# Layer 3 of a four-layer kernel: PSUM banks divided 5/1/2 in place of 4/1/3, parameters in smaller steps, attention begun beside the first sequence's parameters

## The chip, the cores and the metric

The kernel runs on one core of one Trainium2 chip. The core has the engines PE (TensorE, matrix products; its weight loads are listed as PEld), DVE (VectorE), ACT (ScalarE), POOL (GpSimd) and SP (SyncE, which issues DMAs here). Each engine works through its own list of instructions in order and waits on semaphores for the others. Matrix products land in PSUM, which this program divides into eight banks of 128 x 512 f32; DVE and ACT read them from there.

The metric is the device time of one execution in microseconds (us). Before the change it is 3640.95 us, the median of three runs (3640.08 to 3649.79).

## The reference, cut to what matters

The kernel computes four layers, each `x = x + s * silu(ffn)`. The change touches layer 3 alone. It takes 8 sequences of 512 tokens with 128 features and computes two branches from the same normalized input:

```
xn = layernorm(x)
# branch s: state space mixer, 4 heads of 64, state 128
z, x, B, C, dt, A, trap, angles = split(xn @ W_in)
a = min(-softplus(A), -1e-4); dt = softplus(dt + dt_bias)
theta = cumsum(angles * dt)                 # over tokens
K = rope(rmsnorm(B) + B_bias, theta); Q = rope(rmsnorm(C) + C_bias, theta)
y = within a chunk: (Q K^T * g * decay) x  +  Q exp(ell) state   # plus D * x
s = (y * silu(z)) @ W_out
# branch ffn: attention, 16 heads of 8
attn = softmax over queries of (k q^T / sqrt(128)); out = sum_k attn * v
f = gelu(l2norm(l2norm(out @ Wo) @ Wff))
x = x + s * silu(f)
```

## The kernel before

Layer 3 works through the sequences one after another. A sequence has T = 512 tokens, JT = 4 tiles of 128.

**Attention in units.** A unit is one group of four heads (of four groups) and one tile of 128 keys, so a sequence has U = 16 units. `scores` makes four products of 128 x 512 on PE (L1957), each into a PSUM bank of the kind `pu`; DVE takes each product's negative maximum (`nm`, L1960), ACT its exponential with the sum of a row (L1961). Two units later (LAG = 2) `weigh` takes the reciprocal of the sums on DVE (L1934), scales the values on POOL (L1935) and makes four products into the single `pf` bank (L1942). After the fourth key tile of a group, the result is copied to `oT`.

**The mixer.** `mixer(b, jt)` handles one tile of 128 tokens. It is a generator of seven steps: (1) the z and x projection (L1849), tanh and copy on ACT, keys and queries with bias on POOL (L1858), rotation on DVE (L1863 to L1865); (2) the decay product (L1870) with four exponentials (L1875) and causal masking on POOL; (3, 4) four transposes each (L1889) and their copies; (5) the product of queries and keys (L1894), multiplied into E by DVE (L1895), and the new state (L1900, L1903 to L1906); (6) the output product with E (L1911) into the first half of the tile `py`, added to y by DVE (L1912), then the product with the state (L1915) into the second half of the same tile, scaled and added (L1917, L1918), times z (L1920); (7) two transposes (L1924) and a copy into `yT`.

**Beginning, parameters, end.** `begin(b)` normalizes, transposes and projects a sequence (L1723 to L1735) and then runs `parameters`, which computes softplus, decays, norms and angles for the whole sequence. Its steps are: two projections of two tiles each (L1754 to L1760); softplus and the products up to L1783; and everything else, from L1788 over the norms (L1800), the dot products (L1804 to L1815) and the cumulative angles (L1819, L1821) to sine and cosine (L1826 to L1839). `end(b)` multiplies by W_out (L1970) and Wo (L1980), normalizes, multiplies by Wff (L1996), applies gelu and writes the result.

**Banks.** The eight banks are divided by `k.banks("l3p", pu=4, pf=1, pa=3)`: four for scores, one for `weigh`, three in turn (`pa`) for all other products.

**What sets the order.** PE's instructions stand in the order in which the program makes them (`manual_schedule` for PE). A scheduler orders those of the other engines by data and priority; scores and weighing are made with high priority (`AHEAD`). The loop in `layer3` runs over the units n. In each it makes the scores, then one step of half of the running generators, then weighs unit n - 2, then one step of the other half:

```
if u == 0 and b + 1 < B:
    running.append(L.begin(b + 1))
mb, mu = divmod(n + HEAD, U)
if mb < B and mu % 4 == 0 and (mb, mu) != (0, 0):
    running.append(L.mixer(mb, mu // 4))
```

`begin(0)` with its parameters runs to its end ahead of the loop. A mixer starts every fourth unit, four units ahead of its place (`HEAD = 4`); `end(b)` starts after the last weighing of its sequence, first in the list.

Of the kernel before, what the change touches and what calls it, by code (L numbers as in the profile page):

```python
# [20 lines left out]
P = 128  # L21
# [1593 lines left out]
def softplus(nc, pool, x):  # L1615

    shape = list(x.shape)
    tl = lambda name: pool.tile(shape, F32, name=name)
    e, z, q, p = tl("sp_e"), tl("sp_z"), tl("sp_q"), tl("sp_p")
    nc.scalar.activation(e, x, AF.Abs)  # L1620
    nc.scalar.activation(e, e, AF.Exp, scale=-1.0)
    nc.vector.tensor_scalar(z, e, 2.0, None, ALU.add)
    nc.vector.reciprocal(z, z)
    nc.vector.tensor_tensor(z, z, e, ALU.mult)
    nc.vector.tensor_tensor(q, z, z, ALU.mult)
    nc.vector.tensor_scalar(p, q, 1.0 / 17, None, ALU.mult)
    for n in range(15, 1, -2):
        nc.vector.scalar_tensor_tensor(p, p, 1.0 / n, q, ALU.add, ALU.mult)
    nc.vector.scalar_tensor_tensor(p, p, 1.0, z, ALU.add, ALU.mult)
    nc.vector.tensor_scalar(x, x, 0.0, None, ALU.max)  # L1630
    nc.vector.scalar_tensor_tensor(x, p, 2.0, x, ALU.mult, ALU.add)


class Layer3:
# [69 lines left out]
    def begin(self, b):  # L1704


        k, nc, cn, fn, tp = self.k, self.k.nc, self.cn, self.fn, self.tp
        bt = slice(b * JT, (b + 1) * JT)
        xn = tp.tile([P, JT, C], F32, name="xn3", bufs=1)
        self.layernorm(self.x[:, bt, :], xn)  # L1710
        yield
        xT = tp.tile([P, T + 1], F32, name="xT3")
        nc.gpsimd.memset(xT[:, T:], 0.0)
        k.to_features(xn, xT, nt=JT)
        yield
# [10 lines left out]
        nc.tensor.matmul(ps, fn["Wq"], xT[:, 0:T], start=True, stop=True)  # L1726
# [12 lines left out]
        yield  # L1739
        yield from self.parameters(q)  # L1740

    def parameters(self, q):
# [8 lines left out]
        for jt in range(JT):  # L1751
            o = slice(jt * P, (jt + 1) * P)
            ps = k.pa()
            nc.tensor.matmul(ps[:, 0 : 256 + NPAR], xT[:, o], cn["bcp"], start=True, stop=True)  # L1754
            c0 = 256 + NPAR
            nc.tensor.matmul(ps[:, c0 + 4 : c0 + 4 + 2 * HM], xT[:, o], self.wm, start=True, stop=True)

            nc.tensor.matmul(ps[:, c0 : c0 + 4], xT[:, jt * P + 1 : (jt + 1) * P + 1], cn["trap"], start=True, stop=True)
            nc.scalar.copy(raw[:, jt].rearrange("p a n -> p (a n)"), ps[:, 0:256])
            nc.vector.tensor_copy(par[:, jt, :], ps[:, 256 : c0 + 4 + 2 * HM])  # L1760
            if jt % 2:
                yield

        beta = sm("beta3", 2, JT, HM)
        nc.scalar.activation(beta[:, 0], par[:, :, 8:12], AF.Tanh, scale=0.5)
# [4 lines left out]
        dt, a = sp[:, 0], sp[:, 1]  # L1770
        nc.vector.tensor_tensor(dt, par[:, :, 0:4], bc(cn["dt_bias"], 1, JT), ALU.add)
        nc.vector.tensor_copy(a, par[:, :, 4:8])
        softplus(nc, self.sp2, sp.rearrange("p a b c -> p (a b c)"))
        ad = ap.tile([P, JT, HM, NA], F32, name="ad3")
        nc.vector.tensor_tensor(ad, bc(par[:, :, 12:44], 2, HM), bc(dt, 3, NA), ALU.mult)
        src = ad.rearrange("p j h n -> p j (h n)")
# [5 lines left out]
        nc.vector.tensor_tensor(v["coef"], dt, beta[:, 1], ALU.mult)  # L1782
        nc.vector.tensor_tensor(v["c"], v["coef"], v["d"], ALU.add)  # L1783
        yield

        ps = k.pa((P, 3, JT * HM))
        for n, tri in enumerate((k.upto, k.above, k.ones)):
# [2 lines left out]
            nc.scalar.activation(flat(v[name]), ps[:, n, :], AF.Exp)  # L1790
        nc.vector.tensor_scalar(flat(v["ell"]), ps[:, 0, :], -1.0, None, ALU.mult)
        nc.vector.tensor_tensor(v["eout"], v["eout"], v["c"], ALU.mult)

        r = self.rms(raw.rearrange("p j a n -> p (j a) n"), 2 * JT, 1e-5)
        rv = r.rearrange("p (j a) -> p j a", a=2)
        BC = tp.tile([P, JT, 2, C], F32, name="BC3")
        nw = cn["nw"].rearrange("p (a n) -> p a n", n=C)
        for jt in range(JT):
            for w in range(2):
                nc.vector.scalar_tensor_tensor(  # L1800
                    BC[:, jt, w, :], raw[:, jt, w, :], rv[:, jt, w : w + 1], nw[:, w, :], ALU.mult, ALU.mult
                )
        prod = ap.tile([P, JT, C], F32, name="prod3")
        nc.vector.tensor_tensor(prod, BC[:, :, 0, :], BC[:, :, 1, :], ALU.mult)  # L1804
        dot = sm("dot3", JT)
# [7 lines left out]

        nc.vector.tensor_tensor(v["coef"], v["coef"], kqd, ALU.mult)
        nc.vector.tensor_tensor(v["coef"], bc(cn["D"], 1, JT), v["coef"], ALU.subtract)  # L1815

        W = JT * HM * NA
        ps = k.pa((P, JT, HM * NA))
# [19 lines left out]
        nc.scalar.activation(n, n, AF.Square)  # L1838
        nc.vector.tensor_scalar(of(cos), n, -2.0, 1.0, ALU.mult, ALU.add)  # L1839
        q.update(v=v, BC=BC, sin=sin, cos=cos, state=None)  # L1840
        q["yT"] = tp.tile([P, 2, JT, P], F32, name="yT3", bufs=1)

    def mixer(self, b, jt):

# [62 lines left out]
            q["state"] = new  # L1907
        yield
        py = k.pa((P, 2, HM, HP))
        for h in range(HM):  # L1910
            nc.tensor.matmul(py[:, 0, h, :], E[:, h, :], xc[:, h, :], start=True, stop=True)  # L1911
        nc.vector.tensor_tensor(y, y, py[:, 0], ALU.add)  # L1912
        if state is not None:
            for h in range(HM):
                nc.tensor.matmul(py[:, 1, h, :], kqT[:, 1, h, :], state[:, h, :], start=True, stop=True)  # L1915
# [12 lines left out]
    def weigh(self, b, u):  # L1928
# [34 lines left out]
    def end(self, b):  # L1963

        k, nc, cn, fn, tp, q = self.k, self.k.nc, self.cn, self.fn, self.tp, self.q.pop(b)
        s = tp.tile([P, JT, C], F32, name="s3", bufs=1)
        ps = k.pa((P, JT, C))
        for jt in range(JT):
            for w in range(2):
                nc.tensor.matmul(  # L1970
                    ps[:, jt, :], q["yT"][:, w, jt, :], cn["W_out"][:, w * C : (w + 1) * C],
                    start=(w == 0), stop=(w == 1),
                )
        nc.scalar.copy(s, ps)
        yield
        z = tp.tile([P, JT, C], F32, name="zo3", bufs=1)
        ps = k.pa((P, JT, C))
        for qt in range(JT):
# [4 lines left out]
                )  # L1983
        nc.scalar.copy(z, ps)
        yield
        r = self.rms(z, JT, 1e-12, floor=True)
        nc.vector.tensor_tensor(z, z, bc(r, 2, C), ALU.mult)
        yield
# [23 lines left out]
def layer3(k, x, A, at):  # L2012

    with ExitStack() as ctx:
        ctx.enter_context(k.banks("l3p", pu=4, pf=1, pa=3))
        L = Layer3(k, ctx, x, A, at, k.out)
        ctx.enter_context(k.tc.manual_schedule(engines={mybir.EngineType.PE}))
        for _ in L.begin(0):
            pass
        U = 4 * JT  # L2020
        AHEAD = 300
        HEAD = 4
        running = [L.mixer(0, 0)]
        for n in range(B * U + LAG):
            b, u = divmod(n, U)
            steps = iter(running)

            def step(share):

                for _ in range(share):  # L2030
                    w = next(steps, None)
                    if w is not None and next(w, False) is False:
                        running.remove(w)

            if b < B:
                if u == 0 and b + 1 < B:
                    running.append(L.begin(b + 1))
                mb, mu = divmod(n + HEAD, U)
                if mb < B and mu % 4 == 0 and (mb, mu) != (0, 0):
                    running.append(L.mixer(mb, mu // 4))  # L2040
                steps = iter(list(running))
                half = (len(running) + 1) // 2
                with k.tc.high_priority(offset=AHEAD):
                    L.scores(b, u)
                step(half)
            else:
                half = 0
            if n >= LAG:
                wb, wu = divmod(n - LAG, U)
                with k.tc.high_priority(offset=AHEAD):  # L2050
                    L.weigh(wb, wu)
                if wu == U - 1:
                    running.insert(0, L.end(wb))
            step(len(running))
        while running:
            for w in list(running):
                if next(w, False) is False:
# [87 lines left out]
```

## Time and profile before

| What | us |
|---|---|
| median of three runs | 3640.95 |
| profiled execution, whole time | 3647.2 |
| span of its records | 3645.5 |
| layer 3, first record of its constants' load to the end | from 2627.5 |
| first score of layer 3 (L1957) starts | 2669.4 |
| last unit's scores start | 3613.4 |

Over the whole span PE is busy 77% of the time, DVE 64%, ACT 45%, POOL 20%; these are means over four different layers. A row of the stage table gives the busy time of each engine in one stretch of the span, and the clock that PE was granted there as a share of full speed. A matmul's end is modelled, so PE's busy time in a group of products includes short waits inside the group. In a wait, the engine that stood is named first, then the one whose work it was waiting for, with the total, the number of times and the longest.

### The profile page before, as it was taken

To read this page: it belongs to the slowest core of one execution; us is meant where nothing else is said; L and a number is where in the kernel's file an instruction comes from. 1 tells how busy PE (TensorE), PEld (TensorE's weight loads), DVE (VectorE), ACT (ScalarE), POOL (GpSimd) and SP (SyncE) were. 2 spreads that over 40 slices of the span, in tenths; PEclk is the share of its full clock that TensorE was granted. 3 is DMA by queue.
4 is the path that set the end of the run, shared out by engine and by line. 5 is a ranking of instruction groups with operands and counts; after the bars stand their busy time and mean duration, and the time that the engine had idled before them with its cause. 6 is when DMAs were issued, how large, how long until landed. Compare 5 with 4: busy or idle time off the path is not lost.

```text
span 3645.5 us, 44996 instructions
## 1 busy us (share of the span) xinstructions
PE 2815.7 (77%) x16390; PEld 1512.3 (41%) x16390; DVE 2315.1 (64%) x6346; ACT 1645.2 (45%) x3211; POOL 743.0 (20%) x845
## 2 busy tenths in 40 slices
PE   6173657512998897799999999999678789887987
PEld 4142445302444454344444444443344445444543
DVE  7989898997582334334544544444467777777775
ACT  5162546512544445233333333333245566665665
POOL 0004040400225553101101101101121222222221
PEclk9585757555789999799999999998868889888988
DMA  4003030311002222000000000000000000000000
GB/s 119 2 2 71 1 82 1 72 48 34 1 2 50 41 39 41 42 1 1 1 1 1 1 1 1 1 1 1 21 1 1 4 4 1 4 3 4 1 4 7
DMA packets 67519, 64.53 MB, mean 18 GB/s; under 512 B 5344, under 2 KB 59616, under 8 KB 66784
## 3 DMA queue, kind: packets, MB, share of 16 engines
q1 hardware_dynamic: 39264, 42.75, 3.8%
q0 software_dynamic: 19712, 14.69, 3.1%
q10 hardware_dynamic: 8320, 4.19, 0.4%
q8 instruction: 129, 2.11, 0.2%
q14 instruction: 94, 0.77, 0.1%
HBM read 43.80 MB, written 17.83 MB: 17 GB/s over the span
## 4 chain that ended last, share of the span: by engine, by line
PE 36%; DVE 17%; ACT 7%; POOL 3%; issue 2%; DMA 1%; POOLq 0%; ACTq 0%; DVEq 0%; SPq 0%
PE pa L1372 6%; PE pu L1390 6%; DVE nm L1960 4%; ACT at L1961 3%; PE pu L1957 3%; PE pf L1942 2%; DVE mpad L1404 2%; PE pf L1435 2%; PE pa L1486 1%; PE pa L1485 1%; PE pa L1870 1%; ACT at L1422 1%; PE pa L1915 1%; DVE rope L1863 1%; PE pa L1509 1%
## 5 line engine op out<-in xcount | busy, mean ns | idle before, releaser
L1961 ACT ACTIVATE at<-pu,nm 128x512 f32<-128x512 f32 x512 | 348.1, 688 | 151.6 <-DVE nm L1960 125.1
L1960 DVE TENSOR_REDUCE nm<-pu 128x1 f32<-128x512 f32 x512 | 326.8, 680 | 66.6 <-PE pu L1957 66.5
L199 POOL TENSOR_SCALAR_AFFINE_SELECT at<-at 128x512 f32<-128x512 f32 x184 | 123.3, 670 | 1004.3 <-ACT at L1422 855.9
L1404 DVE TENSOR_REDUCE mpad<-pu 128x2 f32<-128x256 f32 (+3 forms) x256 | 199.2, 818 | 168.6 <-PE pu L1401 168.6
L1422 ACT ACTIVATE at<-pu 128x1024 f32<-128x1024 f32 (+3 forms) x256 | 171.7, 702 | 285.7 <-PE pu L1390 285.5
L1078 ACT ACTIVATE at<-pu,rsqrt 128x1024 f32<-128x1024 f32 (+3 forms) x256 | 190.9, 793 | 190.1 <-PE pu L1073 164.4
L1957 PE MATMUL pu<-qT,kT 32*128 32x512 f32 x1024 | 246.4, 703 | 6.0 <-ACT at L1961 5.1
L1372 PE MATMUL pa<-hid,f 128*128 128x512 f32 x512 | 222.7, 593 | 0.0
L1390 PE MATMUL pu<-qT,kT 32*128 32x512 f32 (+3 forms) x1024 | 160.8, 516 | 56.4 <-DVE mpad L1404 42.0
L748 PE MATMUL pa<-ident,Y 128*128 128x128 f32 x32 | 7.9, 426 | 210.9 <-DVE Y L739 210.9
L1390 PE MATMUL pu<-kT,qT 32*128 32x128 f32 (+3 forms) x1024 | 151.8, 569 | 14.4 <-ACT at L1422 10.2
L1942 PE MATMUL pf<-at,va 128*32 128x512 f32 x1024 | 158.9, 698 | 1.4 <-POOL va L1935 1.4
L548 POOL DMA_INDIRECT xg<-xn_d,idx x48 | 54.9, 1143 | 496.9 <-PE pf L552 316.3
L1372 PEld LDWEIGHTS pa<-hid,f 128*128 128x128 f32 x512 | 96.6, 190 | 119.5 <-issue 118.9
L1493 DVE SCALAR_TENSOR_TENSOR X<-X,u 128x512 f32<-128x512 f32 x56 | 38.7, 691 | 159.5 <-ACT u L1488 159.5
L1073 PE MATMUL pu<-qT,kT 32*128 32x512 f32 (+3 forms) x1024 | 131.1, 518 | 5.7 <-ACT at L1078 4.7
L1390 PEld LDWEIGHTS pu<-qT,kT 32*128 32x128 f32 x1024 | 67.5, 197 | 155.5 <-DVE mpad L1404 116.3
L1016 POOL DMA_INDIRECT f_d<-ys,idx x64 | 103.6, 1619 | 138.0 <-DMA f_d<-ys,idx 86.0
L1935 POOL TENSOR_TENSOR va<-V,sm 128x32 f32<-128x32 f32 x128 | 38.8, 303 | 451.7 <-DVE sm L1934 401.5
L1957 PEld LDWEIGHTS pu<-qT,kT 32*128 32x128 f32 x1024 | 81.9, 209 | 103.2 <-ACT at L1961 65.5
L1373 ACT ACTIVATE hid<-pa,f 128x512 f32<-128x512 f32 x64 | 44.0, 688 | 172.5 <-PE pa L1372 172.5
L1083 DVE TENSOR_TENSOR at<-at,ceiling 128x512 f32<-128x512 f32 x72 | 50.2, 698 | 108.2 <-ACT at L1078 104.8
(611 smaller groups left out, 6723.3 us busy)
## 6 DMA issues: line engine op xcount, KB each, us to landing
w<-in_w_dram SPq DMA_DIRECT2D x24, 512.0 KB, 3.8
f_d<-zeros ACTq DMA_DIRECT2D x8, 512.0 KB
xn_d<-xn SPq DMA_DIRECT2D x8, 512.0 KB, 4.9
w<-in_w_dram SPq DMA_DIRECT2D x16, 256.0 KB, 2.9
w<-in_w_dram SPq DMA_DIRECT2D x24, 128.0 KB
f<-in_f_dram SPq DMA_DIRECT2D x1, 2888.0 KB, 11.8
xn<-in_x_dram SPq DMA_DIRECT2D x4, 512.0 KB, 9.3
Gt<-in_x_dram SPq DMA_DIRECT2D x4, 512.0 KB
```

Of the source, the lines that this page charges most:

```text
L199: self.nc.gpsimd.affine_select(a, a if src is None else src, pattern, ALU.is_ge, 0.0, base=0, channel_multiplier=-1)
L1016: nc.gpsimd.indirect_dma_start(out=self.f_d, out_offset=bass.IndirectOffsetOnAxis(ap=idx[:, e, i : i + 1], axis=0), in_=ys[:, i, :], in_of ...
L1073: nc.tensor.matmul(pu[:, n, 0:m], q["kT"][r, g // 2, kc * P : kc * P + P], q["qT"][r, g, kc * P :], start=True, stop=True,)
L1078: nc.scalar.activation(at_[:, i : i + 2, 0:m], pu[:, :, 0:m], AF.Square, bias=k.rsqrt2, scale=32.0**-0.5)
L1372: nc.tensor.matmul(ps, fn[n][:, c0 : c0 + P], src[:, i, :], start=(i == 0), stop=(i == 3))
L1390: self.k.nc.tensor.matmul(pu[:, n, 0:m], a[r, c0 : c0 + P], b[r, q0 : q0 + m], start=True, stop=stop)
L1404: nc.vector.tensor_reduce(top[:, i : i + 2, 16], pu[:, :, 0:m], AX.X, ALU.max)
L1422: nc.scalar.activation(at_[:, i : i + 2, 0:m], pu[:, :, 0:m], AF.Exp, scale=8.0**-0.5)
L1942: nc.tensor.matmul(po[i * 32 : i * 32 + 32, :], va[:, kc, c0 : c0 + 32], E[:, i, :], start=(kc == 0), stop=(kc == JT - 1))
L1957: nc.tensor.matmul(pu, q["kT"][r, kc * P : (kc + 1) * P], q["qT"][r, g, :], start=True, stop=True)
L1960: nc.vector.tensor_reduce(nm[:, w], pu, AX.X, ALU.max, negate=True)
L1961: nc.scalar.activation(E[:, n, :], pu, AF.Exp, bias=nm[:, w], accum_out=sm[:, w])
```

## The change

Nothing is added to or taken from the computation. What is different:

- the banks are divided `pu=5, pf=1, pa=2`: scores go round five banks, the other products round two;
- `parameters` has more steps: softplus is a generator that yields after its two ACT instructions, further yields follow softplus, the products, the decays, half of and all of the norms, and the dot products; the reciprocal root for the norms (`rms`) is taken before softplus;
- in the mixer the product with the state comes ahead of the one with E; `yT` is allocated in the first mixer's last step in place of at the end of `parameters`;
- `end` makes the Wo product first, then waits until the last mixer has set `mixed`, then makes the W_out product;
- the loop starts as soon as the first sequence's projections stand (`ready`); the parameters of sequence 0 run as a generator beside the first units. Mixers are planned by `at`: from unit 10 on every third unit until they have caught up with their place, then every fourth, one unit ahead of it. `begin(b)` is planned for the later of the sequence's usual place and 16 units ahead of its first mixer, and not before the mixers that read its buffers.

```diff
     nc.scalar.activation(e, e, AF.Exp, scale=-1.0)
+    yield
     nc.vector.tensor_scalar(z, e, 2.0, None, ALU.add)
...
         yield
+        q["ready"] = True
         yield from self.parameters(q)
...
             if jt % 2:
                 yield
+        r = self.rms(raw.rearrange("p j a n -> p (j a) n"), 2 * JT, 1e-5)
...
-        softplus(nc, self.sp2, sp.rearrange("p a b c -> p (a b c)"))
+        yield from softplus(nc, self.sp2, sp.rearrange("p a b c -> p (a b c)"))
+        yield
...
         nc.vector.tensor_tensor(v["c"], v["coef"], v["d"], ALU.add)
+        yield
         yield
...
-        r = self.rms(raw.rearrange("p j a n -> p (j a) n"), 2 * JT, 1e-5)
+        yield
...
+            if jt == 1:
+                yield
+        yield
         prod = ap.tile([P, JT, C], F32, name="prod3")
...
         nc.vector.tensor_tensor(v["coef"], bc(cn["D"], 1, JT), v["coef"], ALU.subtract)
+        yield
...
-        q["yT"] = tp.tile([P, 2, JT, P], F32, name="yT3", bufs=1)
...
         py = k.pa((P, 2, HM, HP))
+        if state is not None:
+            for h in range(HM):
+                nc.tensor.matmul(py[:, 1, h, :], kqT[:, 1, h, :], state[:, h, :], start=True, stop=True)
         for h in range(HM):
             nc.tensor.matmul(py[:, 0, h, :], E[:, h, :], xc[:, h, :], start=True, stop=True)
         nc.vector.tensor_tensor(y, y, py[:, 0], ALU.add)
         if state is not None:
-            for h in range(HM):
-                nc.tensor.matmul(py[:, 1, h, :], kqT[:, 1, h, :], state[:, h, :], start=True, stop=True)
             inter = tl("inter3", HM, HP)
...
+        if jt == 0:
+            q["yT"] = self.tp.tile([P, 2, JT, P], F32, name="yT3", bufs=1)
...
         nc.scalar.copy(q["yT"][:, :, jt, :], ps)
+        q["mixed"] = jt
...
-        ctx.enter_context(k.banks("l3p", pu=4, pf=1, pa=3))
+        ctx.enter_context(k.banks("l3p", pu=5, pf=1, pa=2))
...
+        EARLY, EVERY = 10, 3
+        at = lambda b, jt: max(b * U + jt * JT - 1, EARLY + EVERY * (b * JT + jt))
...
+        for b in range(B):
+            if b:
+
+                read = at(b - 2, JT - 1) + 1 if b > 1 else 0
+                plan(max((b - 1) * U, at(b, 0) - U, read), lambda b=b: L.begin(b))
+            for jt in range(JT):
+                plan(at(b, jt), lambda b=b, jt=jt: L.mixer(b, jt))
+            plan(max((b + 1) * U + LAG, at(b, JT - 1) + 1), lambda b=b: L.end(b))
+        running = [L.begin(0)]
+        while not L.q or "ready" not in L.q[0]:
+            next(running[0])
+        for n in range(B * U + LAG + 1):
+            running.extend(make() for make in work.get(n, ()))
```

In `end` the W_out product and its copy move behind the Wo product, after

```diff
+        while q.get("mixed") != JT - 1:
+            yield
```

More of the change, by code (lines that the diff above doesn't have):

```diff
@@ L1965, in end @@
         k, nc, cn, fn, tp, q = self.k, self.k.nc, self.cn, self.fn, self.tp, self.q.pop(b)
[L1966 to L1975, printed above, removed]
         z = tp.tile([P, JT, C], F32, name="zo3", bufs=1)
@@ L1985, in end @@
         yield
+        while q.get("mixed") != JT - 1:
+            yield
+        s = tp.tile([P, JT, C], F32, name="s3", bufs=1)
+        ps = k.pa((P, JT, C))
+        for jt in range(JT):
+            for w in range(2):
+                nc.tensor.matmul(
+                    ps[:, jt, :], q["yT"][:, w, jt, :], cn["W_out"][:, w * C : (w + 1) * C],
+                    start=(w == 0), stop=(w == 1),
+                )
+        nc.scalar.copy(s, ps)
         r = self.rms(z, JT, 1e-12, floor=True)
@@ L2014, in layer3 @@
     with ExitStack() as ctx:
-        ctx.enter_context(k.banks("l3p", pu=4, pf=1, pa=3))
+        ctx.enter_context(k.banks("l3p", pu=5, pf=1, pa=2))
         L = Layer3(k, ctx, x, A, at, k.out)
         ctx.enter_context(k.tc.manual_schedule(engines={mybir.EngineType.PE}))
-        for _ in L.begin(0):
-            pass
         U = 4 * JT
         AHEAD = 300
[L2022 to L2026, printed above, removed]
+        EARLY, EVERY = 10, 3
@@ new lines, in layer3, with plan @@
+        at = lambda b, jt: max(b * U + jt * JT - 1, EARLY + EVERY * (b * JT + jt))
+        work = {}
+        def plan(n, make):
+            work.setdefault(n, []).append(make)
+        for b in range(B):
+            if b:
+                read = at(b - 2, JT - 1) + 1 if b > 1 else 0
+                plan(max((b - 1) * U, at(b, 0) - U, read), lambda b=b: L.begin(b))
+            for jt in range(JT):
+                plan(at(b, jt), lambda b=b, jt=jt: L.mixer(b, jt))
+            plan(max((b + 1) * U + LAG, at(b, JT - 1) + 1), lambda b=b: L.end(b))
@@ L2028, in step @@
+        running = [L.begin(0)]
[3 more added lines that the diff above has]
+            running.extend(make() for make in work.get(n, ()))
+            todo = list(running)
             def step(share):
-                for _ in range(share):
-                    w = next(steps, None)
-                    if w is not None and next(w, False) is False:
+                for w in todo[:share]:
+                    if next(w, False) is False:
@@ L2033, in step @@
                         running.remove(w)
[L2035 to L2042, printed above, removed]
-                with k.tc.high_priority(offset=AHEAD):
[L2044 to L2047, printed above, removed]
@@ L2048, in layer3 @@
-            if n >= LAG:
-                wb, wu = divmod(n - LAG, U)
+                del todo[:share]
+            if n < B * U:
+                with k.tc.high_priority(offset=AHEAD):
+                    L.scores(*divmod(n, U))
+                step((len(todo) + 1) // 2)
+            if LAG <= n < B * U + LAG:
                 with k.tc.high_priority(offset=AHEAD):
[L2051 to L2054, printed above, removed]
+                    L.weigh(*divmod(n - LAG, U))
@@ L2055, in layer3 @@
+            step(len(todo))
         while running:
```

## The prediction

> **What bounds the kernel now.** The change touches layer 3 alone, so I first looked for its stage. The stage table (busy us of each engine in stretches of the span) was read for the start of the layer, for one ordinary sequence and for the last one. Its columns are the stretch and its length, then busy time of PE, PEld, DVE, ACT and POOL, then granted clock, DMA share and GB/s.
>
> ```profile
> 2642.30:2669.40 27.10, 9.86 (x45) 7.27 (x43) 16.52 (x55) 5.83 (x15) 6.96 (x4) 0.62 0.00 0
> ...
> 2906.00:3024.00 118.00, 101.56 (x554) 54.17 (x554) 87.42 (x209) 75.15 (x192) 25.95 (x39) 0.84 0.01 3
> ...
> 3497.00:3616.00 119.00, 108.31 (x593) 55.44 (x594) 79.25 (x164) 73.55 (x201) 22.87 (x39) 0.88 0.01 3
> ```
>
> Between the first projections (2642.3) and the first score (2669.4) lie 27.1 us of parameters with no attention beside them. Each sequence then takes about 118 us for 16 units, 7.4 us a unit, and no engine is full: DVE 87 of 118, ACT 75, PE 102 at a clock of 0.84. The last sequence has no following parameters, less DVE work, and takes 119 all the same. So DVE's throughput is not the bound; waits that pass between engines are. The waits of the stage (2669.4 to 3616; total us, times, longest):
>
> ```profile
> PEld pu L1957 <- ACT at L1961: 65.5, 117, 3.3
> ...
> PE pa L1915 <- DVE y L1912: 50.1, 24, 3.3
> ...
> PE pa L1894 <- DVE coef L1814: 40.8, 3, 13.6
> ...
> PE pa L1849 <- DVE angle L1829: 29.0, 3, 9.8
> ```
>
> PE, whose order is the program's, stands 120 us at the last three places; the first line is its weight load for a score, which waits until an exponential frees the bank. What follows such a stand is seen in PE's timeline (start, us, line, operation; idle before it in brackets):
>
> ```profile
> 3062.30 1.13 PE L1726 MATMUL pa<-xT,f 128*128 128x512 f32 x2 [0.47 <-ACT s L1974]
> ...
> 3076.97 1.10 PE L1900 MATMUL pa<-xe,kq 128*128 128x64 f32 x8 [0.60 <-DVE par L1760]
> ...
> 3530.31 1.16 PE L1870 MATMUL pa<-upto,adt 128*128 128x128 f32 x8
> ...
> 3584.57 1.97 PE L1915 MATMUL pa<-state,kqT 128*128 128x64 f32 x8 [1.08 <-DVE y L1912]
> 3586.47 1.94 PE L1942 MATMUL pf<-at,va 128*32 128x512 f32 x8
> 3588.34 2.08 PE L1870 MATMUL pa<-upto,adt 128*128 128x128 f32 x8
> ```
>
> L1870 takes 1.16 us where PE did not stand, 2.08 soon after it did.
>
> **The change, part by part.** The instructions of PE, DVE and POOL are the same in number; only order and banks move.
>
> *A, earlier start.* Once qT and kT stand, the first scores are behind only two parameter tiles, at about 2645 in place of 2669.4: 24 us. The parameters' 16.5 us of DVE move beside units 0 to 9, which carry no mixer and need DVE 4 x 0.61 + 0.18 = 2.6 us each. The mixers postponed follow every third unit until unit 43, so their work is later, not gone. If DVE were the bound only its idle 27.1 - 16.5 = 10.6 us would be won, if nothing were, 24. Take **18**.
>
> *B, state product ahead of E product (L1915 before L1911).* Both write the tile py. Before, PE writes the first half, DVE reads it (L1912), and only then may PE write the second half. In the new order PE writes both and DVE comes after: the wait goes, 24 times 2.1 = 50 us. Late next is the product with E, whose input is made a unit earlier, and the transpose of y, which needs four DVE operations of about 0.41 (L1912, L1917, L1918, L1920), 1.6 us; between py and it PE has weights (1.06), a transpose group (0.66) and scores (1.1), 2.8 us, unless four maxima of 0.61 come first: 0 to 1 us each. The slow clock behind the stand: over the 24 places L1915 itself ran 11.8 us above 1.10 each, the L1942 after it 13 above 1.06, the L1870 15 above 1.13: 40 us. [...] The rows say 50 + 40 = 90, with half speed after gaps of 1.1 to 3.3 us. I use the rows, but not all of it: DVE and ACT do other work during the stand and have to keep up afterwards. **60**, bounds 25 and 90.
>
> *C, parameters in steps of a unit.* Before, everything from L1788 to the angles is one step; PE then finds a bank held by the angles' product until L1829 or a transpose not copied. That step's stands, all six of them, in the stage table (first two):
>
> ```profile
> 2859.50:2873.20 13.70, 0.07 (x5) 0.06 (x1) 12.25 (x31) 8.39 (x14) 2.36 (x3) 0.65 0.04 11
> 2985.90:2995.20 9.30, 0.00 (x0) 0.00 (x0) 8.18 (x19) 3.92 (x10) 3.68 (x3) 0.72 0.00 0
> ...
> sum 69.80, PE 0.10 PEld 0.12 DVE 61.99 ACT 37.33 POOL 19.66; mean PE 0.02 PEld 0.02 DVE 10.33 ACT 6.22 POOL 3.28
> ```
>
> PE does nothing for 69.8 us, but DVE works 62 of these, and that work remains. Spread over five units, with the softplus ahead of it over three, it must fit into the 31 us that DVE idles in a sequence. At least DVE's 8 us are won, at most 70. Take **35**.
>
> *D, fifth score bank.* A score then waits for an exponential five back, not four: 0.67 us earlier (688 ns of L1961 overlapping its 201 ns read). The 117 waits are 0.56 us on average, so nearly all 65.5 could go; but there ACT's four exponentials (2.7 us) set the pace in light units whatever the banks. **15**, bounds 0 and 50.
>
> *E, two banks for other products in place of three.* The stage takes 360 such tiles: 32 mixers x 7 + 24 state tiles = 248, beginnings 32, parameters 48, ends 32. With three banks PE's plain waits for them are small: 6.1 + 3.5 + 2.6 + 1.8 us in all (L1870 on xv, L1900 on par, L1754 on y, L1726 on s). With two, each tile waits for the last reader of the second before it. In the new PE order that is, in a mixer: the new state's product (L1900) behind z's tile (its readers tanh, DVE, copy ended 3.0 us after PE at 3550; 3.3 us of PE work lie between: 0 to 2); the decay product L1870 behind L1894's reader L1895 (0.68 alone, ended 3.2 us after PE at 3547; 1.0 us of PE between: 0 to 2.2). Take 0.5 each: 12 + 16 us. Parameter tiles in pairs 1 us, 16 in all: 16; the angles' tile 1.5 x 8 = 12; the tile of q with four readers of 0.7, 1.5 x 8 = 12. Sum 68. Queued behind each on PE are the next scores, for which DVE and ACT wait; half of it falls where PE would have waited for a score bank. **-35**, bounds 0 and -110.
>
> [...] The rows of short waits (0.47 and 0.60 us above) are followed by 1.13 and 1.10 us, full speed. [...]
>
> *F, small.* In the changed program's order ACT loads tables 36 times in the stage, before 40 times, 1.28 us each; off the path mostly: 2. At the end zo's product no longer stands behind s's (1.9 us), but the last mixer runs three units later with its transpose ahead: 0. Moving yT's allocation and the rms forward moves one POOL power of 1.64 us to an earlier unit; POOL is busy 26 of 118. No DMA is added; the one per sequence on SP moves with the ends.
>
> Sum: 18 + 60 + 35 + 15 - 35 + 2 = 95. The profiled execution took 3647.2 us (span 3645.5), so 3552; the median of the runs shown is 6 lower, 3641, and from it **3546**.
>
> **Rivals.** *R1, DVE becomes the bound:* the parameters' work only moves. A 10, B 25, C 8, D 0, E -20: 23 us, **3618**. For it: DVE works 90% of the stands. Against: 31 us idle a sequence, and the last sequence is no faster with 8 us less.
>
> *R2, the pair of banks becomes the bound, slower.* Place: L1870 and L1900 in each mixer, then the parameter tiles. It decides once the mean new wait is over 128 / 360 = 0.36 us a tile, since A to D and F give 130. Price at the upper ends: 32 x 2.2 + 24 x 1.5 + 40 of the others = 146, and slow groups after a third of them (30 us): 176 - 130 = 46 over, **3687**. For it: copies queue behind high priority maxima. Against: tiles of one mixer are mostly a unit apart.
>
> *R3, the stands go and nothing replaces them:* DVE's 715 us of the 1003 us from 2642 to the end (sums of the stage table) at 85% gives 841, 162 less: **3479**. For it: PE's work at full clock is an estimated 86 us a sequence, from the fast rows: scores 16 x 1.1, weights 16 x 1.06, mixers 4 x 7.6, end 7.7, parameters 9.3, beginning 4. Against: E.
>
> *R4, gains and new waits cancel:* within 11 us of 3641.
>
> **Chances.** Forecast 0.40 (own range 3505 to 3595), R3 0.20, R1 0.17, R4 0.05, R2 0.18. No change is within 0.3%, 11 us. Faster 0.76, same 0.06, slower 0.18. The range 3470 to 3660 leaves out about 0.05 below and 0.13 above.
>
> **What would show it.** A: first score near 2645. B: no wait of L1915's product for L1912, L1870 near 1.1. C: no PE gap above 4 us, DVE above 80% in a sequence. D: score waits below 40 us. E: waits of PE on ACT and DVE readers of pa tiles, 70 us in sum; above 150 I am wrong and R2 holds. Sequences should fall to about 108 us; if they stay near 115 with DVE full, R1.

## The result, and the profile after

| | median, us | lowest to highest, us | runs |
|---|---|---|---|
| before | 3644.61 | 3640.08 to 3662.48 | 14 |
| after | 3633.83 | 3626.53 to 3640.16 | 14 |

The ratio is 0.9966, 95% interval 0.9956 to 0.9977: faster by 0.34%, some 12 us. The forecast was 3546 us, 95 us faster. The sign was right and the time lies inside the range, but seven eighths of the gain are missing.

The stage table of the kernel after, with the columns of the one shown of before; the first stretch now contains the first units, the last row begins where the scores run out:

```profile
2645.00:2763.00 118.00, 93.75 (x456) 41.73 (x455) 93.56 (x243) 74.39 (x203) 26.05 (x38) 0.83 0.00 1
...
3117.00:3235.00 118.00, 89.98 (x488) 50.33 (x488) 83.69 (x192) 69.32 (x172) 23.51 (x35) 0.79 0.01 3
...
3471.00:3589.00 118.00, 96.58 (x608) 50.70 (x600) 90.06 (x181) 76.56 (x203) 26.34 (x41) 0.92 0.01 3
```

The middle row has the fewest matmuls of the seven whole stretches behind the first, which have 488 to 608; the row of before that the prediction shows had 554. PE was busy for 90 us in it, in that row of before for 102: it stands more. DVE is not full either (84 of 118).

A clearer measure is the time from the first score of one sequence to the first score of the next. Before, the first sequence took 130.1 us and the next six 117.8 to 122.5. After, the first takes 97.8 and the next six 120.4 to 134.9, where the forecast had about 108. So the layer is 56 us ahead when the second sequence's scores begin, and loses 39 of these behind that. A part of the loss is work put off, because mixers of the first sequences now run in later ones. But in the fourth to the seventh sequence, where the mixers have caught up (from unit 43 on), a sequence takes 126.5 us on average, where before it took 120.0. In these profiles the kernel after is the slower one, apart from its beginning.

Where PE stands, the table of PE's waits in layer 3 says (waiting instruction, what it waited for, us in total, times, longest):

```profile
PE pa L1857 <- DVE E L1903: 28.8, 8, 5.6
PE pa L1736 <- DVE E L1903: 19.6, 4, 4.9
PE pa L1878 <- DVE E L1903: 17.7, 8, 4.2
PE pa L1935 <- DVE y L1929: 12.8, 7, 3.4
...
PE pa L1756 <- ACT yT L1936: 9.9, 5, 2.0
...
PE pa L1920 <- ACT E L1883: 1.0, 1, 1.0
```

The last line is what is left of the 50.1 us in 24 stands of the state product: that wait is gone, as are the 40.8 and 29.0 us of L1894 and L1849. In their place PE waits for E at L1903, the DVE operation that multiplies the key-query product into E and so releases its bank: 77.4 us in 23 stands if all lines of that kind are added. Stands of all kinds add up to 204 us of layer 3, where before had 171. Two expected things did happen. The first score starts at 2646.6 us, where it was 2669.4. And a score's weight load waits less for an exponential, 23.4 us in place of 65.5:

```profile
PEld pu L1969 <- ACT at L1973: 23.4, 43, 2.1
```

One of the new stands in the timeline of after (start, us, engine and line, operation; idle before it in brackets):

```profile
3152.76 1.00 PE L1908 MATMUL pa<-xe,kq 128*128 128x64 f32 x8
3153.05 1.28 DVE L1972 TENSOR_REDUCE nm<-pu 128x1 f32<-128x512 f32 x2
...
3154.32 0.69 DVE L1972 TENSOR_REDUCE nm<-pu 128x1 f32<-128x512 f32 x1
3154.49 1.02 POOL L1702 TENSOR_TENSOR rs<-ss,minus_half 128x4 f32<-128x4 f32 x1 [7.56 <-DVE ss L1698]
3155.48 2.00 POOL L1866 TENSOR_TENSOR kq<-BC,c 128x1024 f32<-128x1024 f32 x1
3155.54 2.49 DVE L2000 TENSOR_TENSOR zo<-zo,rs 128x512 f32<-128x512 f32 x1 [0.54 <-POOL rs L1702]
3157.95 0.68 DVE L1903 TENSOR_TENSOR E<-E,pa 128x512 f32<-128x512 f32 x1
...
3158.68 2.07 PE L1736 MATMUL pa<-f,xT 128*128 128x128 f32 x8 [4.92 <-DVE E L1903]
```

The two tiles before the stand are the key-query product (L1902) and the new state (L1908). The next one, the values of a beginning sequence (L1736), needs the older of the two banks. Its reader L1903 takes only 0.68 us, but on DVE there are maxima ahead of it, and then `zo` of a sequence's end, which itself waits for POOL. With a third bank, L1736 would have had somewhere else to go: in the version with 4/1/3 below, no wait of L1736 for L1903 is left. Behind the stand it takes 2.07 us for eight matmuls of 128x128; the eight of L1902, ahead of the stand, took 1.16. The granted clock was 1.00 up to 3158.6, where the stand ends, and 0.50 behind it.

### The profile page after: what moved, and what is told of

The parts are those of the page before. It is cut to its first block, busy times and chain, and to the rows that moved or that the text cites. A ratio compares the mean times of both kernels' runs of the same rounds, so it can differ in the third digit from the quotient of the medians.

```text
span 3629.3 us, 44988 instructions
## 1 busy us (share of the span) xinstructions
PE 2764.3 (76%) x16390; PEld 1479.4 (41%) x16390; DVE 2336.2 (64%) x6346; ACT 1642.4 (45%) x3207; POOL 745.4 (21%) x845
## 4 chain that ended last, share of the span: by engine, by line
PE 35%; DVE 16%; ACT 7%; issue 2%; POOL 2%; DMA 0%; POOLq 0%; ACTq 0%; DVEq 0%; SPq 0%
PE pa L1372 6%; PE pu L1390 6%; DVE nm L1972 4%; ACT at L1973 3%; PE pu L1969 3%; PE pf L1954 2%; DVE mpad L1404 2%; PE pf L1435 2%; PE pa L1486 1%; PE pa L1485 1%; ACT at L1422 1%; PE pa L1878 1%; PE pa L1509 1%; PE pa L1359 1%; PE pa L1515 1%
## 5 line engine op out<-in xcount | busy, mean ns | idle before, releaser
L1969 PE MATMUL pu<-qT,kT 32*128 32x512 f32 x1024 | 203.1, 731 | 2.4 <-ACT at L1973 2.3
L1390 PEld LDWEIGHTS pu<-qT,kT 32*128 32x128 f32 x1024 | 67.3, 196 | 154.4 <-DVE mpad L1404 114.3
L700 DVE TENSOR_TENSOR Z<-Hs,KE 128x96 f32<-128x96 f32 x510 | 108.8, 253 | 0.9
```

Source lines behind the costliest of these rows:

```text
L700: nc.vector.tensor_tensor(z[:, 0:3, v, :], bc(prev[:, v, :], 1, 3), bc(KE[:, o + t, 0:3, :], 2, 4), ALU.mult)
L1390: self.k.nc.tensor.matmul(pu[:, n, 0:m], a[r, c0 : c0 + P], b[r, q0 : q0 + m], start=True, stop=stop)
L1969: nc.tensor.matmul(pu, q["kT"][r, kc * P : (kc + 1) * P], q["qT"][r, g, :], start=True, stop=True)
```

## The experiments

All ratios are to the kernel before, run on the same chip beside it, with a 95% interval. Letters A to F are the parts of the forecast; "4/1/3" is the division of the banks (scores, weighing, others). Line numbers in an experiment's profile are its own: near those of after where it is made from the change, near those of before elsewhere.

### Two banks or three

The change with the old division of banks:

```diff
-        ctx.enter_context(k.banks("l3p", pu=5, pf=1, pa=2))
+        ctx.enter_context(k.banks("l3p", pu=4, pf=1, pa=3))
```

> The changed kernel with the banks of before: four for scores, one, three for the other products. Theory T1 (two banks ate the gain): PE's stands on readers of pa tiles, about 200 us in the changed kernel, fall below 60, score waits come back by some 40 us, and the time falls to about 3570 (3530 to 3600). Rival T2 (DVE and its contention with POOL set the pace of a unit, 736 us busy in the stage against 715; the stands are only where PE waits for it): the stands move to the score banks and the time stays at 3634, within 12.

Measured: 3591.24 us, **0.9856** (0.9835 to 0.9876). The time is near that of T1, though PE's stands on `pa` tiles fell from 201 to 93 us only, and not below 60. The same with `pu=4, pf=1, pa=2`, one bank unused, so that the lost third bank stands apart from the fifth score bank:

> The changed kernel with four score banks and two for the others, one bank left unused. It shows the fifth score bank alone: against the changed kernel the time rises by what that bank is worth. T1 with the fifth bank worth what its waits fell by (PE's weight loads for scores waited 65 us before, 23 after): 3660 to 3680. T2: within 12 of 3634.

Measured: 3639.68 us, **0.9991** (0.9983 to 0.9999). That is far less than T1 had for the fifth bank. With four score banks and two for the others, the weight loads of scores wait 45.8 us for exponentials (83.2 with 4/1/3), so the fifth bank takes away 22 us of such waits and not 42, and 9 us of time. And the kernel before, with 5/1/2 and nothing else:

> The kernel before with five score banks and two for the other products, nothing else. T1: PE's new waits on readers of pa tiles appear here too, 150 us or more, less some 40 for scores: 3700 to 3760. T2: 3645, within 15.

Measured: 3683.93 us, **1.0109** (1.0093 to 1.0126), which is between T1 and T2. So the third bank is worth 0.0135, 49 us, inside the change; the fifth score bank gives back 0.0025, 9 us; and in the kernel before the exchange of the one for the other costs 40 us. In the waits of the change with 4/1/3, those for L1903 are down to 23.9 us in 14 stands:

```profile
PE pa L1897 <- DVE kq L1873: 24.1, 4, 9.0
PE pa L1935 <- DVE sm L1946: 17.4, 4, 4.6
...
PE pa L1994 <- DVE E L1903: 11.9, 4, 3.0
```

Is it that one tile, or two banks as such? Here the key-query product has a bank of its own, and two banks are in turn for the rest:

```diff
-        ps = k.pa((P, HM, P))
+        ps = k.psum("px", (P, HM, P))
...
+        ctx.enter_context(k.banks("l3p", pu=4, pf=1, pa=2, px=1))
```

> The changed kernel with four score banks, two banks in turn for the other products, and the eighth bank for the key-query product alone (the tile that DVE's E* operation reads). Theory H (the two banks cost what they cost because that one tile is held while E* stands in DVE's queue): as good as three banks in turn, ratio 0.983 to 0.988, and the PE waits for E* nearly gone from the table of waits. Theory G (any tile of two in turn is held long enough, whichever it is): hardly better than two banks in turn with one bank unused (0.9991), 0.994 to 0.999, the waits spread over the other readers. Between them, 0.988 to 0.994: the tile is a part of the cost.

Measured: 3607.03 us, **0.9927** (0.9913 to 0.994). No wait for L1903 is left in its table, yet only 0.0064 of the 0.0135 come back, 23 us of 49. The rest has moved to the tiles that stay in the pair:

```profile
PE pa L1994 <- DVE state L1911: 13.5, 4, 3.4
PE pa L1935 <- DVE y L1929: 12.2, 7, 2.7
PE pa L1920 <- DVE state L1914: 10.1, 4, 3.0
```

The key-query tile is thus about half of the price in this order of PE's work, and a pair of banks as such the other half.

### The state product

The kernel before, with the order of the two output products alone exchanged (B):

```diff
         py = k.pa((P, 2, HM, HP))
+        if state is not None:
+            for h in range(HM):
+                nc.tensor.matmul(py[:, 1, h, :], kqT[:, 1, h, :], state[:, h, :], start=True, stop=True)
         for h in range(HM):
             nc.tensor.matmul(py[:, 0, h, :], E[:, h, :], xc[:, h, :], start=True, stop=True)
...
-            for h in range(HM):
-                nc.tensor.matmul(py[:, 1, h, :], kqT[:, 1, h, :], state[:, h, :], start=True, stop=True)
```

> The kernel before with the product with the state ahead of the one with E, nothing else. The wait of 50 us for L1912 goes. By the prediction's term B the time falls by 60 to 3585 (3555 to 3620). T2: DVE and ACT work on during the stand, so little is won: 3630 to 3645.

Measured: 3576.74 us, **0.9816** (0.98 to 0.9831). These lines alone give 67 us, more than five times the whole change. The other way round, the change with this part alone undone:

> The changed kernel (banks 5/1/2) with the old order of the two output products: E first, DVE's addition, then the state. If the state product first is worth as much in the changed kernel as alone in the one before (65 us): 3699 (3685 to 3710). If PE's stands on the two banks cover that wait: 3634 to 3650.

Measured: 3686.89 us, **1.0143** (1.0125 to 1.0161): without B the change is slower than before by 52 us. The stand is back, in the waits of that kernel:

```profile
PE pa L1923 <- DVE y L1920: 62.3, 24, 7.2
```

What follows a stand can be seen in the durations of single matmuls (shortest, median and longest in ns). The state product before:

```profile
L1915 PE MATMUL pa<-state,kqT x192: 275/421/476, 2724.3 to 3607.8; 128*128 128x64 f32 x192
```

and after:

```profile
L1920 PE MATMUL pa<-state,kqT x192: 275/275/476, 2762.5 to 3603.5; 128*128 128x64 f32 x192
```

The median went from near the slow end to the fast one. Was it the stand that made these matmuls slow, or was PE slow already? PE's timeline of before has both (L1911 is the product with E, ahead of the stand):

```profile
2782.46 1.10 PE L1911 MATMUL pa<-xc,E 128*128 128x64 f32 x8
2785.71 1.97 PE L1915 MATMUL pa<-state,kqT 128*128 128x64 f32 x8 [2.14 <-DVE y L1912]
2787.61 1.94 PE L1942 MATMUL pf<-at,va 128*32 128x512 f32 x8
...
3581.52 1.97 PE L1911 MATMUL pa<-xc,E 128*128 128x64 f32 x8
```

In the first place the granted clock was 1.00 up to 2785.1 and 0.50 from 2785.2 to 2792.0. Of the 24 stands, 18 began at a granted clock of 1.00. Behind 15 of these, of 1.33 to 3.29 us, the clock fell to 0.50 within 4.4 us of the stand's beginning; behind three, of 2.29 to 2.43 us, it did not. The other six began at 0.50 already. The last line belongs to one of them, the stand of 1.08 us that the prediction shows. At 19 of the 24 places the state product took more than 1.10 us; at 13 of these the clock fell between the stand's beginning and the product's end, at six it was 0.50 before the stand. Over the layer, B alone takes the time at half clock from 328 to 253 us.

### Early start and small steps, one at a time

On top of the change with 4/1/3 (0.9856), the early start undone: mixers planned from unit 0, and

```diff
-        while not L.q or "ready" not in L.q[0]:
-            next(running[0])
+        for _ in running.pop():
+            pass
```

> The changed kernel with banks 4/1/3 and without the early start: the first sequence's parameters run to their end ahead of the first score, as before. Against the changed kernel with 4/1/3 (3591): if the early start is worth the 20 us by which the first score comes earlier, 3611 (3605 to 3618); if those units only grow longer, 3591.

Measured: 3597.81 us, **0.9895** (0.9881 to 0.991), so there the early start is worth 0.0039, 14 us. The other one has the old large steps (all yields that the change adds to `parameters` and `softplus` taken out, the rms back in its old place):

> The changed kernel with banks 4/1/3 and the parameters' old, large steps (rms late, softplus in one); early start and late mixers stay. The kernel before with only the state product first took 3577, the changed one with 4/1/3 took 3591, though it has the early start as well: something in it costs about 34. Theory T3, the small steps are what costs (their small DVE operations stand between the maxima, DVE is busy 22 us more): 3557 (3545 to 3572). Rival T4, the mixers' start three units later costs: 3591 (within 10). My prediction's term C (small steps win 35): 3620.

Measured: 3599.31 us, **0.9899** (0.9886 to 0.9913): small steps are worth 0.0043, 16 us, in that surrounding.

Now the sum is odd: B alone gave 0.9816, and B with A and C, at the same division of banks, 0.9856. Something in the change takes away what A and C bring. Two suspects, first the mixers, which start one unit ahead in the change and four before (the state product first, `HEAD = 1`, and the last sequence's end at the back of the list):

> The kernel before with the state product first (3577 of 3642, ratio 0.982) and mixers started one unit ahead of their place instead of four; nothing else. The early start is worth 0.4% and the small steps 0.4% in the changed kernel with banks 4/1/3, and yet that one stands at 0.986; so something else in it costs about 1.2%. T4 (the later mixers cost it): ratio 0.993, 3615. Rival T5 (the order within a unit: ends last in the list, Wo product first): ratio 0.982, 3577.

Measured: 3580.36 us, **0.9825** (0.9811 to 0.9838). Then the place of a sequence's end in the list of running work; the change with 4/1/3 and

```diff
-            running.extend(make() for make in work.get(n, ()))
+            for make in work.get(n, ()):
+                w = make()
+                running.insert(0 if w.__name__ == "end" else len(running), w)
```

> The changed kernel with banks 4/1/3 (ratio 0.986), where an end joins the running generators at the front of the list as before, not at its end. T4: unchanged, 0.983 to 0.988. T5: most of the 1.2% comes back, 0.975.

Measured: 3586.96 us, **0.9844** (0.9831 to 0.9857, as good as unchanged). Neither suspect explains the gap alone. A version with the early start, the old large steps, mixers four units ahead and two buffers for `yT` does not fit: a pool of its buffers needs 32.25 kb a partition, and 30.78 were left. Two mixtures with 4/1/3, the early start, ends in front with both products in one step and mixers four units ahead (`b * U + jt * JT - 4`), with large and with small steps:

> Banks 4/1/3, state product first, early start, the parameters' old large steps (with the late mixers these took ratio 0.990), mixers four units ahead, ends at the front with both products in one step. T4: 0.990 - 0.012 = 0.978. T5: also 0.978. If early start and state product don't add up: 0.982 or more.

> As the last, but with the parameters in small steps, three fewer than in the changed kernel so that they end four units before the sequence does and mixers can start four units ahead. If state product first (-1.8%), early start (-0.4%), small steps (-0.4%) and early mixers add up: ratio 0.974, 3545. T6 (units are then bound by DVE, so the parts no longer add up): 0.980 or more.

Measured: 3589.33 us, **0.9851** (0.9836 to 0.9866), and 3609.85 us, **0.9905** (0.989 to 0.9921). Here small steps cost 0.0054 where above they gained 0.0043.

### One edit at a time over the state product

So each remaining edit was laid over the state product alone. The early start only (mixers at `max(4 * i - 4, 5 + 3 * i)`):

> The kernel before with the state product first (0.9816 measured) and only the early start of the change laid over it: scores of unit 0 once the first sequence's queries and values are there, mixers at unit 5 + 3i until these meet the old places at 4i - 4. Parameters in the old large steps, ends as before, four banks and three. If the parts add up: 14 us less, 0.978, which would beat every version so far. If the postponed mixers and the first sequence's parameters pay it back later, as they seemed to in the changed kernel: 0.981 to 0.986.

Measured: 3570.51 us, **0.9823** (0.9809 to 0.9836): nothing over 0.9816, though its first score starts 9.5 us after the layer's first product, where that version's starts 34.3 after it. The lead is gone when the third sequence's scores begin: 263.8 us after the layer's first product here, 263.2 there. Over the version with mixers one unit ahead (0.9825), the small steps only:

> The same (0.9825 measured) with the parameters in the changed kernel's small steps, and nothing else. Theory S (small steps cost in the steady state what they save in the first sequences): 0.987 to 0.992. Theory Q2 (they cost nothing): 0.980 to 0.984. My own sum gave small steps a gain of 35 us, which would be 0.973.

Measured: 3570.64 us, **0.9818** (0.9805 to 0.9832): nothing. Over the same one, the order in `end` only, Wo's product first and W_out's after the yield. As in the change, this also drops the yield behind the second product, so that an end has one step fewer; the two were not run apart.

> The kernel before with the state product first and mixers begun one unit ahead (0.9825 measured), and a sequence's end in the changed kernel's order: the Wo product first, then W_out. Theory P (the changed order of the ends is what keeps the changed kernel with three banks behind the state product alone): 0.988 to 0.992. Theory Q (it is not the ends): 0.981 to 0.984.

Measured: 3532.41 us, **0.9722** (0.9709 to 0.9736). An edit that I had priced at nothing gives 37 us, and this version beats both kernels, by 0.0278 and 0.0244 of the time before (101 and 89 us). Is that gain a property of the edit? Three neighbours of this version, each with one thing different: the small parameter steps; the ends at the back of the list; the mixers four units ahead.

> The state product first, mixers one unit ahead, the Wo product first in each end (0.9722 measured), and now the change's small parameter steps too. It is then the changed kernel with three banks and without the early start, but for the place of a sequence's end in the list of running work (that one measured 0.9895). Theory S2 (small steps break what the order of the ends brings: the transposes wait for the key-query scaling on DVE, 47 us in 8 waits in the trace of e18): 0.980 to 0.990. Theory V (the ends' place at the back of the list does it): 0.970 to 0.975 here.

> The version with 0.9722 measured, and only this moved: each sequence's end stands at the back of the list of running work and not at its front, so that in each unit it is stepped after the mixers and the parameters, as in the changed kernel. Theory V (the place of the ends): 0.982 to 0.992. Theory S2 (the small steps): 0.970 to 0.975.

> The kernel before with the state product first and the ends' two products exchanged, mixers four units ahead as before: the two edits alone. If the exchange is a gain of its own (37 us at one unit ahead): 0.970 to 0.974, against 0.9816 for the state product first alone. If it was a lucky fit of the steps at one unit ahead: 0.979 to 0.984.

Measured: 3578.54 us, **0.9841** (0.9827 to 0.9856); 3585.79 us, **0.9867** (0.9852 to 0.9882); 3585.97 us, **0.9861** (0.9844 to 0.9877). Each takes 43 to 53 us away again, more than the edit had brought, and neither theory that named one culprit holds. The last one is slower even than its two ranges allowed. The waits of the version at 0.9722 and of its neighbour with the ends at the back show what differs. The former:

```profile
PE pa L1788 <- DVE adt L1779: 52.8, 7, 9.2
PE pa L1788 <- DVE c L1783: 17.0, 1, 17.0
PE pu L1958 <- ACT at L1962: 11.3, 9, 3.3
```

The latter:

```profile
PE pa L1849 <- DVE angle L1829: 22.7, 3, 8.2
PE pa L1889 <- ACT xv L1855: 21.9, 5, 4.8
PE pa L1981 <- DVE E L1895: 17.8, 6, 3.0
PE pa L1849 <- DVE E L1895: 17.7, 4, 5.4
```

In the first, most of PE's stands (70 of 112 us) are where a sequence's parameters need them, at the product that sums the decays: 7 plus 1 stands at L1788, as many as there are sequences. In the second it stands less there and, besides, wherever the next tile of the round finds a bank whose reader is late on DVE or ACT. The likely reading is that one step moved inside a unit shifts the round of three banks and so which products meet such readers; no run tests it by itself.

## Why the prediction was wrong

Each row is layer 3 in one profile of a kernel, in us from its first product to the end. Stands are PE's waits behind that product. The next column is the time for which PE's granted clock was 0.50. The last is the mean of the fourth to the seventh sequence, from first score to first score.

| kernel | layer 3 | PE busy | PE's stands | half clock | DVE busy | a sequence |
|---|---|---|---|---|---|---|
| before | 1010.3 | 827.2 | 170.8 | 327.6 | 717.9 | 120.0 |
| after | 993.2 | 777.6 | 203.6 | 279.8 | 740.2 | 126.5 |
| change with 4/1/3 | 946.7 | 826.7 | 108.1 | 288.0 | 736.9 | 116.5 |
| change with 4/1/2 | 1000.3 | 811.3 | 176.7 | 307.4 | 738.5 | 125.4 |
| own bank for the key-query tile | 980.9 | 820.2 | 148.6 | 301.6 | 738.1 | 122.0 |
| state product first alone | 942.8 | 798.1 | 132.4 | 253.3 | 716.8 | 111.5 |
| and mixers one ahead, ends exchanged | 908.0 | 783.3 | 112.5 | 198.1 | 719.9 | 105.8 |
| the last, with the ends at the back | 958.9 | 801.6 | 145.6 | 255.8 | 722.0 | 114.6 |

What is left of layer 3 beside PE's busy time and its stands is 12 us in each row, 11 of it behind PE's last product. So the time is PE's work with its slow clock and short waits inside groups (both count as busy) plus its stands. R1 falls with the table too: with nearly the same DVE work, 717 to 722 us, the layer takes anything from 908 to 1010. A profile is one execution; that of the change with 4/1/3 was the fastest of five, 15 us under their median.

The way from before to after, by medians, in parts of 3642 us: B alone -67 us (0.9816); then A, C, the order of the ends and the later mixers together +15 (0.9856); then the third bank taken away +49 (0.9991); then a fifth score bank -9 (0.9966). That is -12.

Against the terms of my sum:

- **B, 60: right.** 67 alone, 64 inside the change (1.0143 to 0.9966), between the 50 of the stands alone and the 90 that the rows said. In the table PE's stands fall by 38 us with B alone and its busy time by 29, where the rows had 50 and 40. The granted clock of before bears the rows out in part: behind 15 of the 24 stands, of 1.33 to 3.29 us, it fell from 1.00 to 0.50. But at six of the 24 places PE was at 0.50 ahead of the stand already, so the 40 counted too much, and half speed "after gaps of 1.1" was a misreading: the stand of 1.08 us is one of these six, and the shortest behind which the clock fell was 1.33 us.
- **D, 15: near.** 9. The waits fell below 40 us as said, but only the 22 us between 4/1/2 and the change belong to this bank.
- **A, 18, and C, 35: where the sum failed first.** The step that failed is adding A and C to B as gains that stay. Over the state product alone, each gives nothing (0.9823 on 0.9816; C over B with mixers one unit ahead, 0.9818 on 0.9825), and all that the change does beside B at three banks costs 15 us. With F's 2 I had +55 for this: 70 of the 83 missing us. Read in the surrounding of the change with 4/1/3, A gives 14 and C 16, so C was sized at twice its worth there: I had counted a stall of PE under which DVE worked 62 of 70 us as half won. The profiles show where the gains went. A's lead of 25 us is given back within two sequences, where the parameters of the first one and the mixers put off now run. And with C, A and the rest at three banks, PE's stands do fall, by 24 us (132.4 to 108.1), but its busy time for the same products rises by 29 (798.1 to 826.7), with 288 us at half clock in place of 253. The sum had put that at nothing.
- **E, -35: the second.** It is -49, inside the bounds: 14 us more. The place named was too narrow. L1878 and L1908 do wait for the key-query tile's reader (17.7 and 6.4 us), but most of the price falls on the product that happens to come next in PE's list, z's projection (28.8) or a beginning (19.6). I had priced that reader by what ends 3.2 us after PE at one place, and not by the queue of maxima, parameters and ends that may stand ahead of it on DVE: single stands reach 5.6 us, against 2.2.
- **F, order of the ends at 0: wrong.** By its surrounding, it takes 37 us off (0.9825 to 0.9722) or adds 16 (0.9816 to 0.9861, where the last sequence's end also moves to the back of the list). The step fewer in each end is part of both.

D's 6 us too many and B's 7 too few make up the rest of 83. By my own test (waits on readers of `pa` tiles above 150 us) rival R2 should hold. It named the right place, and the sum of its stands was passed, but not its sign: a stand that is new in PE's list replaces in part one that was there, and the sum of stands rose by 33 us only. R2's 30 us for slow groups after a third of the new waits were an estimate (32 groups at 0.92 us, the difference of the two L1870 in the prediction's rows, come to as much), and no run shows them: from three banks to two (4/1/3 to 4/1/2) the time at half clock rises by 19 us, but PE's busy time falls by 15.

Part of what small steps cost is visible. In the four pairs of versions that differ in the steps alone, the time at half clock rises with small steps by 5, 12, 51 and 51 us and PE's busy time by 17, 12, 20 and 21, while its stands change by -39, -20, -3 and +20. The times of these pairs changed by -0.0043, -0.0007, +0.0054 and +0.0119: the same edit went both ways. Why PE is at half clock for longer with them is not shown. DVE's busy time rises too, by up to 25 us, but DVE is not what bounds the layer.

Which rule decides where the round of banks falls well stays open. Fourteen versions with B and 4/1/3 ran, between 0.9722 and 0.9905, and a single moved step changed the ratio by up to 0.0145. So a term that was read from one pair of versions alone, as D, E and its two halves were, may hold some of this.

## What to carry to other kernels

Where PE's order is fixed and banks go round in turn, do not add up gains of separate edits: first find the stand that is there whatever the order (here two products into one tile with a reader between them, 67 us from moving three lines), take it alone, and measure every further edit over it. Before taking a bank from a round, look for the tile whose reader can be held up longest in its engine's queue; its holding time, not the reader's own duration, is the price (here PE stood 4.92 us at a bank whose reader takes 0.68). And when steps are moved inside such a round, allow for a change either way (here up to 1.4% from one moved step), try a few neighbours, and keep the best measured one rather than the best argued.

## What was unexpected of the hardware

A DVE operation took several times its own duration beside POOL here. `zo` times its factor takes 692 to 693 ns at all eight places before; after (shortest, median, longest in ns):

```profile
L2000 DVE TENSOR_TENSOR zo<-zo,rs x8: 693/2482/2486, 2799.5 to 3613.9; 128x512 f32<-128x512 f32 x8
```

In the timeline shown it starts 0.06 us after POOL's addition L1866, which takes 2.00 us, and ends 0.55 us after that one, somewhat less than its own 0.69. Five of the eight `zo` start so, 0.06 to 0.07 us after an L1866, and take 2.48 to 2.49 us; the three that run beside no L1866 take 0.69 to 0.73. The same shows on a tiny operation: L1629 has a median of 181 ns, and its four longest, of 1.79 to 1.80 us, each start 0.25 us after an L1866; one that starts 0.18 us after an L1866 takes 0.19. What makes the difference the records do not show. No price for it was in my sum; the eight `zo` took 14.5 us together, 9 more than eight times 0.69, and in the stand shown 1.8 us of it lie straight ahead of the reader that PE was waiting for.
